# Two-way instead of four-way interleaving of a chunk's columns, and layer 1 in batches of eight blocks

## The chip, the cores and the metric

The kernel runs on one core of one Trainium2 chip. Its time is device microseconds (us) of that core. TensorE (PE) multiplies, VectorE (DVE) and ScalarE (ACT) do the elementwise work, GpSimd (POOL) does a few powers and adds, and SyncE (SP) issues the transfers. "PEld" in the profile is TensorE's loading of weights, the stationary operand of a matmul.

## What is computed

There are 4096 nodes with 64 features, and a dense adjacency matrix of 4096 x 4096 float32 (64 MB) of which somewhat under one entry in a hundred is not zero. Cut to what matters:

```python
# layer 0, two hops
h = relu(layernorm(x)); g = h
for k in range(2):
    g = tanh(concat([adj @ g, g], axis=1) @ W[k])
x = x + g
# layer 1
h = relu(layernorm(x))
mask = adj != 0
rank = cumsum(mask, axis=1); deg = rank[:, -1:]; k = minimum(deg, 100)
w = mask * where(rank - (deg - k) > 0, 0.5 ** (deg - rank), 0)
x = x + w @ (h @ weight) + bias
```

So layer 0 needs the matrix twice (once for each hop), and layer 1 needs, for each entry that is not zero, how many such entries stand to its right in its row.

## The kernel before, in words

**Chunks, blocks and the order of columns.** The rows of the matrix are cut into four *row chunks* of 1024 (I, or g, or J where it is the source of layer 1), and its columns into 32 *blocks* of 128 source nodes. The host lays the matrix out so that `adjA[I, b]` is one transfer of 128 source nodes by 1024 target nodes of chunk I, 512 KB. On the chip the 1024 target nodes of a chunk are two halves of 512 columns (c). A half holds four *tiles* t of 128 nodes, and its column number is 4 p + t for node p of tile t: the four tiles are interleaved. A chunk's features stand in two forms: transposed, 128 partitions (half, feature) by 512 columns in that order, and by nodes. Going from the first to the second is a transpose on TensorE: `nodes` (L198) takes each tile's 128 columns out of the transposed form as the weights of a matmul against the identity (L202). In memory the columns of a tile are thus four float32 elements apart. The way back is `features_T` (L249), whose copy `hT` (L258) writes with the same step. `nodes` is called eight times: for x1 of each chunk in the first sweep, in `finish_row` (L297), and for x2 of each chunk in the second, in `finish_x2` (L409).

**Sweep 1** (L325) reads the whole matrix for the first hop. DVE also makes of every block a byte code per entry (`count_pair`, L211), which stays on the chip, and the aggregation runs as `agg_pair` (L232) or, for blocks whose second hop can be done from the same read, as full-width matmuls (L362).

**Sweep 2** (L611) reads the rest of the matrix again for the second hop (L658 to L660). In the stretch that matters here it reads into four slots of `ring`, so a block's transfer can start only when the block four places before it has been multiplied. A block costs two matmuls of `agg_pair`, side by side in the two halves of the array's columns.

**Layer 1** runs in between and after. Its work is 64 *units* (J, g, n), in the order of `units` (L463): source chunk J = 3, 2, 1, 0, target chunk g = 0 to 3, and n = 0 to 3 for pairs of source blocks. Each unit is first decoded to bf16 powers of two: `convert` (L468) widens its bytes, on ACT (two of L488) or on DVE (L479 and L482), and `add_base` adds a row of counts on DVE (L501). Then `layer1(n)` (L532) takes n units: for all of them the matmuls with the high parts of the features (L549, weights 128 wide, four for each unit), and then for all of them those with the low part (L560, weights 64 wide in the two column halves, four for each unit). It is called with 2. The sums of four units (one J and g) gather in one accumulator of PSUM, and after the fourth `layer1` reads it out: for J = 3 with copies (L572), for J = 2 and 1 with three adds on DVE (L578), for J = 0 with three adds into temporaries (L586), which `finish_out` (L592) multiplies with the weights (L193, "pf"), copies (L596), transposes by nodes (L602, "pto"), adds to the residual (L607) and stores. In layer 1 the two halves of a unit's columns are the even and the odd ones, so L602 picks columns two elements apart. The temporaries come from a pool of five buffers.

**What sets the order.** All engines work in program order, and the program is written out by a planner: `clock` (L388) holds an estimated time of each engine, `decode` (L513) issues conversions and adds as long as their engine's clock is at most `lead` ahead of TensorE's, and `due` (L635) says how many units are to be done after so many blocks of sweep 2, so that 36 of the 64 are due by its end. `while state["done"] + 2 <= due(n + 2)` (L674) issues batches between the blocks; L696 to L698 does so after the last block. The lead is 5.0 in the sweep, 2.5 after it and 8.0 once chunk 0 of x2 is ready (L683 to L686). `finish_x2` (L394) makes a chunk's features for layer 1 in steps: matmul (L193), add and tanh, transpose (L202), residual (L410), layer norm (L152 to L163, with a power on POOL, L158), split into bf16 parts (L425 to L429). Units of source chunk J wait for that of chunk J.

Of the kernel before, what the change touches and what calls it, by code (L numbers as in the profile page):

```python
# [16 lines left out]
P = 128  # L17
# [14 lines left out]
def gnn_kernel(  # L32
# [21 lines left out]
    nc = tc.nc  # L54
# [4 lines left out]
    CB = 8  # L59
    NCH = NB // CB  # L60
# [3 lines left out]
    TC = C // P  # L64
# [31 lines left out]
    def tmp(shape=None, dtype=F32, name="tmp"):  # L96
        return tpool.tile(shape or [P, C], dtype, tag="tmp", name=name)

    def one(name="one"):
        return pone.tile([P, C], F32, tag="one", name=name)  # L100

    def two(name="two"):
        return pone.tile([P, C], F32, tag="two", name=name)
# [26 lines left out]
    ident = cpool.tile([P, P], F32, name="ident")  # L130
# [53 lines left out]
            nc.scalar.activation(hx[:, b0 + i, :D], xc[:, i, :], AF.Relu, scale=s[:, i : i + 1])  # L184


    by_t = lambda ap: ap.rearrange("q (p t) -> q t p", t=TC)

    def paired(po, terms):

        for n, (w, v) in enumerate(terms):
            for c in range(NC):
                nc.tensor.matmul(  # L193
                    po[c * D : (c + 1) * D, :], w(c), v(c),
                    start=n == 0, stop=n == len(terms) - 1,
                )

    def nodes(src):  # L198

        pt = one(name="pt")  # L200
        for t in range(TC):
            nc.tensor.matmul(  # L202
                pt[:, t * P : (t + 1) * P], by_t(src)[:, t, :], ident,
                start=True, stop=True, skip_group_check=True,
            )
        return pt.rearrange("p (t c e) -> p t c e", t=TC, c=NC)
# [33 lines left out]
    def step():  # L240
        while steps:
            try:
                next(steps[0])
                return
            except StopIteration:
                steps.pop(0)


    def features_T(I):  # L249
        pt = one(name="ph")  # L250
        for t in range(TC):
            for c in range(NC):
                nc.tensor.matmul(
                    pt[c * D : (c + 1) * D, t * P : (t + 1) * P],
                    hx[:, CB * I + c * TC + t, :D], ident, start=True, stop=True, skip_group_check=True,
                )
        hT = tmp(name="hT")
        nc.scalar.copy(by_t(hT), pt.rearrange("q (t p) -> q t p", t=TC))  # L258
        return hT

    def own_share(I):
# [7 lines left out]
    def finish_row(I, acc, held):  # L269
# [25 lines left out]
        nc.scalar.activation(x1T, x1T, AF.Tanh)  # L295
        yield
        pt = nodes(x1T)  # L297
        for c in range(NC):
            nc.tensor.matmul(
# [77 lines left out]
    def late_weights():  # L377
        for h in range(2):
            nc.sync.dma_start(wz[h * D : (h + 1) * D, h, 0, 0], weight)
        nc.sync.dma_start(  # L380
            wz[:, 0, 0, 1],
            bass.AP(tensor=bias.tensor, offset=bias.offset, ap=[[0, P], [1, D]]),
        )
# [6 lines left out]
    def use(engine, us, after=0.0):  # L390
        clock[engine] = max(clock[engine], after) + us
        return clock[engine]
# [49 lines left out]
    def space(ap, t=0.0):  # L442
        if not any(ap is g for g in gone):
            spaces.append((ap, t))
# [15 lines left out]
    def ring_space(s):  # L460
        return quad(ring[:, s, :].bitcast(I16))

    units = [(J, g, n) for J in range(NCH - 1, -1, -1) for g in range(NCH) for n in range(CB // 2)]  # L463
    ready = {}
    made = []
    state = {"added": 0, "done": 0, "acc": None, "lead": 5.0}
# [125 lines left out]
    def finish_out(g, ys):  # L592
        po = one(name="pf")
        paired(po, [(lambda c: wa, lambda c: ys[c]), (lambda c: wz[:, c, 0, 0], lambda c: ys[2])])
        oT = tmp(name="oT")
        nc.scalar.copy(oT, po)  # L596
        yield use("ACT", 0.6, use("PE", 1.9) + 0.1)
        pt = two(name="pto")
        v = oT.rearrange("q (c p j) -> q c j p", c=2, j=2)
        for c in range(2):  # L600
            for j in range(2):
                nc.tensor.matmul(  # L602
                    pt[:, (c * 2 + j) * P : (c * 2 + j + 1) * P], v[:, c, j, :], ident,
                    start=True, stop=True, skip_group_check=True,
                )
        o = tmp(name="o")
        nc.vector.tensor_add(o, pt, flat(pre1[:, chunk(g), :]))  # L607
        nc.sync.dma_start(ov[:, chunk(g), :], o.rearrange("p (t e) -> p t e", e=D))
        use("DVE", 0.7, use("PE", 1.3) + 0.2)

    def sweep2():  # L611
        ring_all = list(range(RING))
        early = pacc.tile([P, 3, C], F32, tag="acc", name="acc1")
        accs = {2: early[:, 0, :], 3: early[:, 1, :]}
        plan = [(2, 16, 24), (3, 24, 32), (2, 24, 32), (1, 8, 32), (0, 8, 32)]
        blocks = [(I, b) for I, b0, b1 in plan for b in range(b0, b1)]
        space(quad(mbuf.rearrange("p a r i -> p (a r i)").bitcast(I16)))

        h0_space = hm[:, : 2 * CB, : 2 * D].bitcast(I16).rearrange("p (r k b) d -> p r k b d", r=2, k=2)
        free = {s: 0.0 for s in ring_all}  # L620
        slots = ring_all
        chain = []
        total = len(blocks)
        n_late = 7 * CB // 2

        def run_chain(now):
            if chain and chain[0][0] <= now:
                t, gen = chain.pop(0)
                t = next(gen, None)
                if t is not None:  # L630
                    chain.insert(0, (t, gen))
                return True
            return False

        def due(done_blocks):  # L635

            if done_blocks <= 24:
                return 0
            return (len(units) - n_late) * (done_blocks - 24) / (total - 24)

        seq = 0
        for n in range(0, total, 2):
            I, b = blocks[n]
            if n == 8:
                while steps:
                    step()
                late_weights()
            if n == 24:
                slots = ring_all[:4]
                for s in ring_all[4:]:  # L650
                    space(ring_space(s), free[s])
            if I not in accs:
                accs[I] = two(name="acc1")
            for r in range(2):
                s = slots[seq % len(slots)]
                seq += 1
                a = ring[:, s, :]
                nc.sync.dma_start(a, adjA[I, b + r])  # L658
                landed = use("DMA", 1.33, free[s]) + 2.2
                agg_pair(accs[I], hx[:, b + r, D:], a, b + r == max(CB * I, CB), b + r == NB - 1)  # L660
                free[s] = use("PE", 0.9, landed)
            if steps:
                step()
            if n == 8:
                space(h0_space, clock["PE"])
            if b + 2 == NB and I == 1:
                gone.append(h0_space)
                spaces[:] = [v for v in spaces if v[0] is not h0_space]
            if b + 2 == NB:
                gen = finish_x2(I, accs[I])  # L670
                chain.append((next(gen), gen))
            run_chain(clock["PE"])
            decode()
            while state["done"] + 2 <= due(n + 2):  # L674
                J = units[state["done"]][0]
                if J not in ready or ready[J] > clock["PE"] + 1.0:
                    break
                layer1(2)
                run_chain(clock["PE"])
                decode()  # L680
        for s in slots:
            space(ring_space(s), free[s])
        state["lead"] = 2.5  # L683
        while state["done"] < len(units) or chain or outs:
            if 0 in ready:
                state["lead"] = 8.0  # L686
            if run_chain(clock["PE"]):
                decode()
                continue
            if outs and outs[0][0] <= clock["PE"]:  # L690
                t, gen = outs.pop(0)
                t = next(gen, None)
                if t is not None:
                    outs.insert(0, (t, gen))
                continue
            i = state["done"]  # L696
            if i < len(units) and units[i][0] in ready and ready[units[i][0]] <= clock["PE"] + 1.0:
                layer1(2)  # L698
                decode()
                continue  # L700
            decode()
            later = [x[0] for x in chain[:1] + outs[:1]] + [t for t in ready.values()]
            clock["PE"] = min(t for t in later if t > clock["PE"])

    sweep1()
    sweep2()


# [24 lines left out]
```

## Time and profile before

| | us |
|---|---|
| three runs | 442.91, 443.53, 444.13 |
| median | 443.53 |
| the profiled execution, its own time | 443.52 |
| its span, first to last instruction | 441.7 |
| TensorE busy | 389.2 |
| VectorE busy | 321.9 |
| ScalarE busy | 144.2 |
| granted TensorE clock, mean | 0.954 of full speed |

The span is what the profile's pieces add up to; some 1.8 us of the execution's time lie outside it. Durations below are of this one execution. The "chain of work" is followed back from the last instruction, at each step to what released it, so that its pieces have no gaps between them. In the stage list the columns are the busy time of each engine in a stretch, with the number of instructions in brackets, then the granted clock of TensorE, the share of the transfer engines, and GB/s.

### The profile page before, as it was taken

Reading aid. Unit: us, or ns where it says so; the run is one execution under the profiler, and the core shown is the slowest. Engines: PE = TensorE matmul, PEld = TensorE weight load, DVE = VectorE, ACT = ScalarE, POOL = GpSimd, SP = SyncE. Lnnn points to the kernel's source line nnn. Section 1 sums busy time; section 2 is a strip of 40 time slices with the busy share of each in tenths; the row PEclk is TensorE's granted clock in tenths of the full one; section 3 lists DMA queues with packets and bytes.
Section 4 is the critical chain, followed back from the end, with each engine's and each line's share of the span. In section 5 each row is a group of like instructions: output and inputs, shape, how many; then the busy total and the mean of one; then the engine's idle time right before and its main releaser. Section 6 shows DMA issues by size and latency. Waiting matters only on the chain.

```text
span 441.7 us, 4685 instructions
## 1 busy us (share of the span) xinstructions
PE 389.2 (88%) x1636; PEld 148.4 (34%) x1636; DVE 321.9 (73%) x547; ACT 144.2 (33%) x231; POOL 26.2 (6%) x21
## 2 busy tenths in 40 slices
PE   3748699988999999999979778599999999968995
PEld 0213234312443444444423132333343333422342
DVE  3899965499989997997703045657779999799932
ACT  2134532100120003000043031416457698549810
POOL 1133200000000000000000020030002100020000
PEclk9669989999999999999999898979999999996998
DMA  7999920999999964888499979048866872000011
GB/s 264 409 329 415 406 96 0 347 411 408 410 410 408 407 243 157 302 317 301 160 347 312 391 272 334 16 155 304 299 223 247 281 244 104 2 0 1 0 47 49
DMA packets 31736, 108.54 MB, mean 246 GB/s; under 512 B 4449, under 2 KB 4705, under 8 KB 31713
## 3 DMA queue, kind: packets, MB, share of 16 engines
q1 hardware_dynamic: 31712, 108.25, 65.8%
q8 instruction: 13, 0.21, 0.2%
q14 instruction: 11, 0.08, 0.1%
HBM read 107.18 MB, written 1.05 MB: 245 GB/s over the span
## 4 chain that ended last, share of the span: by engine, by line
PE 70%; DMA 15%; DVE 8%; ACT 3%; POOL 2%; issue 1%; SPq 0%; DVEq 0%; ACTq 0%
PE acc L232 20%; PE acc L362 19%; PE accl L549 12%; DMA ring<-in_adjA_dram 10%; PE accl L560 6%; PE pt L202 4%; PE po L193 3%; DMA codes<-in_adjA_dram 3%; DVE mbuf L215 2%; PE pf L193 2%; DMA pre<-in_x_dram 1%; ACT junk L179 1%; POOL s L181 1%; DVE codes L225 1%; PE pto L602 1%
## 5 line engine op out<-in xcount | busy, mean ns | idle before, releaser
L232 PE MATMUL acc<-ring,hx 128*64 128x512 f32 x456 | 116.5, 639 | 27.2 <-DMA ring<-in_adjA_dram 10.0
L232 PEld LDWEIGHTS acc<-ring,hx 128*64 128x64 f32 x456 | 31.7, 144 | 95.5 <-issue 42.4
L362 PE MATMUL acc<-ring,hx 128*128 128x512 f32 x144 | 62.4, 593 | 0.2 <-DMA ring<-in_adjA_dram 0.2
L232 PE MATMUL acc<-codes,hx 128*64 128x512 f32 x184 | 46.5, 632 | 14.3 <-ACT hx L184 11.4
L225 DVE TENSOR_TENSOR codes<-mbuf,lo 128x512 uint16<-128x512 uint16 x124 | 52.7, 425 | 4.2
L215 DVE TENSOR_SCALAR mbuf<-ring 128x2048 uint8<-128x2048 f32 x37 | 45.2, 1221 | 4.2 <-DMA ring<-in_adjA_dram 4.2
L488 ACT ACTIVATE codes<-codes 128x1024 int16<-128x1024 uint8 x48 | 46.8, 1042 | 1.0 <-PE accl L560 1.0
L226 DVE TENSOR_SCALAR lo<-codes 128x512 uint16<-128x512 uint16 x128 | 37.6, 294 | 4.5
L549 PEld LDWEIGHTS <-hx 128*128 128x128 bf16 x256 | 23.6, 101 | 51.3 <-issue 25.8
L271 ACT COPY S<-acc 128x512 f32<-128x512 f32 x4 | 2.3, 586 | 117.6 <-PE acc L362 116.5
L362 PEld LDWEIGHTS acc<-ring,hx 128*128 128x128 f32 x144 | 27.3, 190 | 34.7 <-issue 33.2
L215 DVE TENSOR_SCALAR mbuf<-codes 128x2048 uint8<-128x2048 f32 x27 | 33.0, 1220 | 7.0 <-DMA codes<-in_adjA_dram 6.9
L501 DVE TENSOR_TENSOR codes<-codes,base 128x2048 uint16<-128x2048 int16 x31 | 36.9, 1220 | 0.1
L158 POOL TENSOR_TENSOR s<-s,half 128x8 f32<-128x8 f32 (+2 forms) x6 | 10.5, 1758 | 338.5 <-DVE s L157 338.5
L549 PE MATMUL accl<-codes,hx 128*128 128x512 bf16 x124 | 30.5, 380 | 0.0
L488 ACT ACTIVATE ring<-codes 128x1024 int16<-128x1024 uint8 x30 | 29.7, 1046 | 0.1
L501 DVE TENSOR_TENSOR ring<-ring,base 128x2048 uint16<-128x2048 int16 x20 | 24.5, 1247 | 5.5 <-ACT ring L488 5.5
L232 PEld LDWEIGHTS acc<-codes,hx 128*64 128x64 f32 x184 | 12.9, 144 | 45.7 <-issue 23.2
L549 PE MATMUL accl<-ring,hx 128*128 128x512 bf16 x80 | 21.6, 405 | 5.7 <-DVE hx L428 5.7
L362 PE MATMUL acc<-codes,hx 128*128 128x512 f32 x48 | 21.2, 594 | 0.0
L560 PEld LDWEIGHTS <-lo 128*64 128x64 bf16 x256 | 11.9, 110 | 20.8 <-issue 13.6
L560 PE MATMUL accl<-codes,lo 128*64 128x512 bf16 x124 | 17.4, 385 | 0.0
(98 smaller groups left out, 331.7 us busy)
## 6 DMA issues: line engine op xcount, KB each, us to landing
ring<-in_adjA_dram SPq DMA_DIRECT2D x146, 512.0 KB, 5.6
codes<-in_adjA_dram SPq DMA_DIRECT2D x54, 512.0 KB, 9.7
xres<-in_x_dram SPq DMA_DIRECT2D x4, 256.0 KB, 6.4
out_dram<-o SPq DMA_DIRECT2D x4, 256.0 KB, 2.5
pre<-in_x_dram SPq DMA_DIRECT2D x3, 256.0 KB, 8.4
pre<-in_x_dram SPq DMA_DIRECT2D x1, 192.0 KB, 6.5
wz<-in_W_dram SPq DMA_DIRECT2D x4, 32.0 KB, 7.3
pre<-in_x_dram SPq DMA_DIRECT2D x1, 64.0 KB, 2.1
```

The lines of the kernel that those rows point to most:

```text
L158: nc.gpsimd.tensor_tensor(s2, s2, half[:, :nb], op=ALU.pow)
L193: nc.tensor.matmul(po[c * D : (c + 1) * D, :], w(c), v(c), start=n == 0, stop=n == len(terms) - 1,)
L202: nc.tensor.matmul(pt[:, t * P : (t + 1) * P], by_t(src)[:, t, :], ident, start=True, stop=True, skip_group_check=True,)
L215: nc.vector.tensor_scalar(m, a, 0.0, float(FLAG - 1), op0=ALU.not_equal, op1=ALU.mult)
L225: nc.vector.tensor_tensor(q, m[:, r].bitcast(U16), cnt, op=ALU.add)
L226: nc.vector.tensor_scalar(cnt, q, 0x7F7F, None, op0=ALU.bitwise_and)
L232: nc.tensor.matmul(acc[c * D : (c + 1) * D, :], src, a[:, c * C : (c + 1) * C], start=first, stop=last,)
L362: nc.tensor.matmul(acc[:, c, :], hx[:, g, :], a[:, r, c * C : (c + 1) * C], start=g == CB * I - 1, stop=g == 0,)
L488: nc.scalar.activation(w[:, r], src[:, r].rearrange("p (x y k) -> p k x y", k=2, x=X), AF.Copy, scale=float(FLAG))
L501: nc.vector.tensor_tensor(w.bitcast(U16), w, bg[:, None, :].to_broadcast([P, 2, CW]), op=ALU.add)
L549: nc.tensor.matmul(like(accs[-1][:, c, :], w), hm[:, CB * J + 2 * k + r, : 2 * D], w[:, r, c], start=k == 0 and r == 0, stop=k == CB // 2 ...
L560: nc.tensor.matmul(like(acc[c * D : (c + 1) * D, 2, :], w), lo[:, CB * J + 2 * k + r, :], w[:, r, c], start=k == 0 and r == 0, stop=k == C ...
```

## The change

The order of columns in a half becomes 256 u + 2 p + v, with tile t = 2 u + v: two tiles are interleaved instead of four. The host's layout of the matrix, `nodes` and `features_T` follow. In layer 1 the even and odd columns then hold, for each, two whole tiles one after the other, so L602 picks columns that stand side by side. For J = 2, 1 and 0 `layer1` is called with four units (eight blocks, all of one J and g) instead of two; for J = 3 still with two. The planner's estimates are unchanged, but it now issues a batch only when four units are due.

```diff
-    by_t = lambda ap: ap.rearrange("q (p t) -> q t p", t=TC)
+    by_t = lambda ap: ap.rearrange("q (u p v) -> q u v p", u=2, v=2)
...
-                pt[:, t * P : (t + 1) * P], by_t(src)[:, t, :], ident,
+                pt[:, t * P : (t + 1) * P], by_t(src)[:, t // 2, t % 2, :], ident,
...
-        nc.scalar.copy(by_t(hT), pt.rearrange("q (t p) -> q t p", t=TC))
+        nc.scalar.copy(by_t(hT), pt.rearrange("q (u v p) -> q u v p", u=2, v=2))
...
-        v = oT.rearrange("q (c p j) -> q c j p", c=2, j=2)
+        v = oT.rearrange("q (c j p) -> q c j p", c=2, j=2)
...
+        def batch():
+            return 2 if units[state["done"]][0] == NCH - 1 else CB // 2
...
-            while state["done"] + 2 <= due(n + 2):
+            while state["done"] < len(units) and state["done"] + batch() <= due(n + 2):
                 J = units[state["done"]][0]
                 if J not in ready or ready[J] > clock["PE"] + 1.0:
                     break
-                layer1(2)
+                layer1(batch())
...
-                layer1(2)
+                layer1(batch())
...
-    adjA = np.asarray(adj).reshape(128, 4, 2, 4, 128, 32).transpose(1, 5, 4, 2, 0, 3)
+    adjA = np.asarray(adj).reshape(128, 4, 2, 2, 2, 128, 32).transpose(1, 6, 5, 2, 3, 0, 4)
```

Built, the changed kernel has as many matmuls, transfers and POOL instructions as before; some conversions move from DVE to ACT. The order on TensorE is the same up to the end of the last batch of J = 3.

## The prediction, made before the changed kernel had run

> **What bounds the kernel now.** I read the page's busy shares and chain first, then the busy times by stage, then the chain piece by piece, then the timelines of VectorE and of the transfers.
>
> ```profile
> PE 389.2 (88%) x1636; PEld 148.4 (34%) x1636; DVE 321.9 (73%) x547; ACT 144.2 (33%) x231; POOL 26.2 (6%) x21
> ...
> PE 70%; DMA 15%; DVE 8%; ACT 3%; POOL 2%; issue 1%; SPq 0%; DVEq 0%; ACTq 0%
> ```
>
> TensorE makes 70% of the chain. The stages from the last quarter of the span on:
>
> ```profile
> core 0: us, PE busy (x) PEld busy (x) DVE busy (x) ACT busy (x) POOL busy (x), PEclk, DMA share, GB/s
> 286.00:320.00 34.00, 33.61 (x162) 11.61 (x164) 23.57 (x35) 15.54 (x19) 3.79 (x2) 0.91 0.71 244
> 320.00:371.00 51.00, 50.94 (x261) 18.68 (x258) 46.71 (x64) 39.57 (x44) 4.46 (x2) 1.00 0.69 240
> 371.00:399.30 28.30, 22.57 (x127) 9.70 (x126) 24.26 (x35) 15.25 (x19) 2.88 (x2) 0.97 0.00 1
> 399.30:437.40 38.10, 37.36 (x192) 15.30 (x192) 25.77 (x31) 19.93 (x23) 0.00 (x0) 0.93 0.06 22
> ```
>
> TensorE is full in all but the third, where it waits some 5.7 us for chunk 0 of x2. But DVE is 46.7 of 51 us busy in the second: it has little room for waits of its own. In the chain, a transpose, the two phases of a batch, blocks, and the next batch:
>
> ```profile
> 328.88 2.06 PE pt L202 x8
> 330.94 1.73 PE accl L549 x8
> 332.66 0.98 PE accl L560 x8
> 333.65 1.72 PE acc L232 x8
> 335.36 1.83 PE accl L549 x8
> ```
>
> (Start, us, what; x8 at L202 is four float32 matmuls of two passes each, at L232 two blocks of 0.86.) The same transpose from weights two elements apart:
>
> ```profile
> 420.49 1.14 PE pto L602 x8
> ```
>
> How DVE waits, and how long two block transfers take that are issued together:
>
> ```profile
> 380.36 1.89 DVE L578 TENSOR_TENSOR codes<-accl,codes 128x512 f32<-128x512 f32 x3 [2.12 <-PE accl L560]
> ```
> ```profile
> ring<-in_adjA_dram SPq DMA_DIRECT2D x1, 512.0 KB, 3.2
> ```
> ```profile
> ring<-in_adjA_dram SPq DMA_DIRECT2D x1, 512.0 KB, 5.4
> ```
>
> L578 stood 2.12 us at the head of DVE's queue until the batch's last L560 was done. The transfers are those issued near 359.1 and 359.9: 3.2 us to landing for the first, 5.4 for the second (4.5 in other pairs).
>
> [...] L202's weight loads take 327 ns, L602's 196, and L362's, contiguous, 190. [...] L549 takes 1.83 after 64-wide work and 1.73 after the 128-wide transpose, so 0.10; L560 takes 0.98 against half of 1.73, so 0.115. [...] after 5.73 idle the batch at 399.27 ran its first eight matmuls in 3.57 instead of 1.83. [...]
>
> **The change part by part.**
>
> *1. Transposes by nodes.* Eight calls, 2.06 to 1.14 each (L602's row, the same shape): -0.92 x 8 = -7.4. All eight lie in the chain. Bounds: 0 if the step isn't what slows them, -7.4.
>
> *2. L602 and hT.* L602's loads go from two elements apart to contiguous: 32 x (196-190) ns = -0.2 at most; taken as 0. hT (1.10 us, 0.59 if contiguous) is waited for by 0.8 us in all; ACT is on the chain there only behind other work. 0, between 0 and -0.8. The host's layout moves the same 512 KB a block: 0. SP and POOL keep their order.
>
> *3. Fewer mode switches.* 48 units in 12 batches instead of 24: 12 x (0.10+0.115) = -2.6. A batch of four costs 5.4 instead of 5.62.
>
> *4. Runs of six blocks on four slots.* The changed order has three runs of six blocks between batches (12 matmuls of L232 in a row), where before no run had more than four. In a run the fifth block's slot is free 0.86 after the start; issue 0.1, 3.2 to landing: there at 4.2, wanted at 3.44. The sixth: free at 1.72, landing 4.5 to 5.4 after issue: 6.3 to 7.2, wanted at 5.0. The run ends at 7.2 to 8.0 instead of 5.16: +2.4 each, +7.3. Before had one such wait, 0.45 at 365. Net +6.9. Were both landings at 3.2, it would be +2.4 in all; at the queue's worst (6.0) +10.
>
> *5. DVE's queue up to chunk 0.* The read-out (L578) of a batch stands in DVE's order ahead of adds (L501, 1.17 each) for the next batch, or the one after. I laid the changed order out by hand, with 5.4 a batch, 0.86 a block, 1.15 a transpose, 1.9 a read-out, 1.17 an add, 0.85 a conversion on DVE, 2.0 on ACT. Zero is the end of the last J = 3 batch (319.96 before). The second J = 2 batch waits for its third and fourth unit (residual and layer norm of x2 stand ahead): +0.95. The next two are supplied. After the sweep three J = 1 batches run on; the third ends at 72.35. Only then can its read-out go (to 74.3), then an add (75.5), L156 and L157 (76.4), two adds (77.6, 78.8): these three adds are the units two to four of the last J = 1 batch, which TensorE had begun at 72.35. It ends at 81.6 instead of 77.75: +3.85. Then its read-out (83.6), one add (84.8), L161, L163, L425, L427, L428: chunk 0 ready at 87.9, 6.3 after the batch against 5.73 before: +0.6. Together +5.4. Nothing covers this: TensorE has no other work then. If DVE's pieces overlap by a fifth it is +4; POOL and DVE together (L161 took 1.1 there) can add 1.
>
> *6. Chunk 0's units.* Before, eight units beyond its own four were added ahead of the first L586, and TensorE ran through: 38.2 us from 399.27 to the last L607. Changed, that L586 stands in DVE's order after the first four units only, and five adds follow it. From chunk 0's readiness: first batch to 7.75 (cold, as before). L586 waits for it, three of 0.63 to 9.75, first add 10.95: TensorE idle 3.2; the second batch takes its units at 1.17 instead of 0.87 each and ends at 17.25. pf to 19.1; the third of the next L586 needs a temporary that pf frees, so the adds come at 20.45, 21.6, 22.8: the third batch ends at 25.5. pto, pf, fourth batch: 34.0. Then pto, pf, oT, pto, pf, oT, pto in a row, two copies of 0.7 exposed: last L607 at 42.6. Net +4.4; this holds 0.9 of the gain of part 3, so +5.3 beside it. Bounds +2 (L586 of the first two columns at the end of the L549 phase; at 380.36 it wasn't so) and +10 (clock, below).
>
> Sum: -7.4 - 2.6 + 6.9 + 5.4 + 5.3 = +7.6. Against the profiled execution, 443.52 (span 441.7 and 1.82 around it; the median of the runs is 443.53): **451.1**, I say 451.
>
> **Rivals.** *A, faster: DVE's queue does not hold TensorE.* Place: read-outs ahead of the next batch's adds, parts 5 and 6. Price without them: -10.0 + 6.9 = 440.4. It decides from parts 5 and 6 together under 3.1 us. For it: before, the same queue kept eight units ahead in the last stage, and the longer waits for blocks give DVE time. Against: strict order, and L578 at 380.36. 0.14.
>
> *B, slower still: the clock.* With 3.2 idle in part 6 and then short bursts, TensorE may fall to half speed for the second and third batches: a unit's four matmuls take 1.72 (0.43 each, as after 399.27) against adds at 1.17, +2.4 each: 456. [...] 0.12.
>
> *C, the change doesn't do what it says:* two elements apart is fast at L602 for another reason and L202 stays at 2.06: +7.4, 458.5. Same engine, operands and shape speak against it. 0.04.
>
> *D, between:* waits of parts 4 to 6 half covered, 443 to 445. 0.04.
>
> **How the numbers follow.** The forecast, parts 1 to 6 as summed, 0.66, with its own range 446.5 to 455: part 4 at +2.4 for the low end, upper bounds of 5 and some of 6 for the high. Leaving out A and C (0.18), the range is 443.5 to 457. Within 0.3% (442.2 to 444.9, about what a measurement of this kernel can tell from no change) is D and a little of the forecast's edge: 0.05. Faster 0.14, slower 0.81.
>
> **What would show it.** L202's weight loads near 196 ns and x8 at 1.14 (part 1, C); L549 and L560 in runs of 16 at about 3.55 and 1.85 (part 3); in three runs of L232 x24 waits on ring loads of 2 to 3 us (part 4); L549 waiting on L501, not on the batch before, before 399 by 4 us, and by 3 us at the second J = 0 batch with DVE idle ahead of L586 (5, 6); the granted clock after it (B). Wrong it would be if waits of L549 on L501 sum to under 3 us, or if DVE is found adding units ahead of the read-outs.

## The result, and the profile after

| | median, us | runs, us | ratio to before, 95% interval |
|---|---|---|---|
| before | 443.65 | 442.91 to 444.13 | |
| changed, first time | 458.3 | 452.63, 458.01, 458.6, 459.25 | 1.0305 [1.022, 1.039] |
| changed, once more | 456.35 | 453.39 to 457.54 | 1.0279 [1.0206, 1.0351] |

The changed kernel is slower by 12 to 15 us, where +7.6 was forecast; 451 was too low and the median lies above the top of the range, 457 (the second median just below it). Some executions are disturbed and come out longer; the medians here and below leave them out, and since the profiled execution of the first time was one of them (461.92; another took 991.84), the profile read here is that of the second: own time 457.53, span 455.0, against 443.52 and 441.7.

The page's busy shares and the chain by engine:

```profile
PE 387.9 (85%) x1636; PEld 143.2 (31%) x1636; DVE 318.3 (70%) x541; ACT 147.8 (32%) x237; POOL 25.4 (6%) x21
...
PE 63%; DMA 19%; DVE 10%; ACT 3%; issue 2%; POOL 1%; SPq 1%; ACTq 0%; DVEq 0%
```

TensorE has hardly less to do (387.9 for 389.2), but it makes 63% of the chain and not 70%; transfers went from 15 to 19% of it, DVE from 8 to 10%, ACT stayed at 3%. Most of the transfers' rise lies ahead of the late stages, in the part of the chain up to 314 us (19% there before, 25% now), so these shares don't say what the change did. The stages do, cut at the same events as before: the end of the last J = 3 batch, the end of the sweep's last block, the first batch of J = 0:

```profile
core 0: us, PE busy (x) PEld busy (x) DVE busy (x) ACT busy (x) POOL busy (x), PEclk, DMA share, GB/s
281.00:315.00 34.00, 32.62 (x162) 11.26 (x164) 24.55 (x37) 16.53 (x20) 3.79 (x2) 0.92 0.69 240
314.90:372.50 57.60, 50.77 (x246) 17.82 (x242) 39.77 (x55) 36.70 (x42) 2.90 (x2) 0.94 0.61 215
372.50:406.80 34.30, 25.41 (x142) 10.82 (x141) 26.48 (x38) 16.06 (x20) 3.79 (x2) 0.93 0.00 1
406.80:450.70 43.90, 38.60 (x192) 16.09 (x192) 27.43 (x31) 27.44 (x31) 0.00 (x0) 0.90 0.05 18
```

In the first column that counts, the length: 51.0 became 57.6, 28.3 became 34.3, 38.1 became 43.9. The last part of the sweep was full (50.94 of 51.00) and now has 6.8 us of gaps, at a clock of 0.94 and not 1.00. The two stages after it have more gaps too. Only the beginning is shorter: the last J = 3 batch ends at 315.1, before at 320.0. One pair of units, 2.8 us of work, also went from the second stage to the third: the second holds 16 units where it held 18.

The chain after the last J = 3 batch, before, and ACT's copy of chunk 1's sums (S, L398) in the same profile:

```profile
319.96 1.72 PE acc L232 x8
321.68 1.83 PE accl L549 x8
323.51 0.98 PE accl L560 x8
324.49 0.95 PE po L193 x4
325.44 3.43 PE acc L232 x16
```
```profile
323.73 0.58 ACT L398 COPY S<-acc 128x512 f32<-128x512 f32 x1
```

The same piece after:

```profile
315.12 0.59 ACT codes L572
...
316.95 2.00 ACT ring L488 x2
318.95 0.48 ACT S L398
319.44 0.04 issue
319.48 5.35 PE acc L232 x16
324.83 0.86 PE po L193 x4
325.69 3.56 PE accl L549 x16
329.25 1.87 PE accl L560 x16
```

Before, this stretch was TensorE without a break. Now the chain leaves it for ACT: read-outs of J = 3, two conversions (L488), and the copy S, which four blocks wait for. These then take 5.35 us; 16 matmuls of L232 took 3.43 before. Below that, a batch of four in 3.56 + 1.87.

The weight loads of four of the transposes by nodes, as a group that keeps shapes apart (operation, count, busy, mean ns of one):

```profile
L202 PEld LDWEIGHTS pt<-ident,y 128*128 128x128 f32 x32 | 4.1, 196 | 2.0 <-issue 1.2 <-ACT y L406 0.8
```

196 ns for a weight load, where L202 had 327. And the DVE queue at the last J = 1 batches and at chunk 0's first read-out (start, us, instruction, in brackets the idle time before and its releaser):

```profile
390.75 1.89 DVE L578 TENSOR_TENSOR codes<-accl,codes 128x512 f32<-128x512 f32 x3 [1.38 <-PE accl L560]
392.56 1.22 DVE L501 TENSOR_TENSOR ring<-ring,base 128x2048 uint16<-128x2048 int16 x1
...
394.48 2.37 DVE L501 TENSOR_TENSOR ring<-ring,base 128x2048 uint16<-128x2048 int16 x2
...
415.10 1.89 DVE L586 TENSOR_TENSOR yo<-accl,codes 128x512 f32<-128x512 f32 x3 [4.30 <-PE accl L560]
416.90 3.49 DVE L501 TENSOR_TENSOR codes<-codes,base 128x2048 uint16<-128x2048 int16 x3
```

DVE stands idle at the head of its queue (1.38, 4.30) while the adds behind it are what TensorE wants next. TensorE's side of these waits, and of the blocks before them:

```profile
346.11 1.08 PE L232 MATMUL acc<-ring,hx 128*64 128x512 f32 x4 [0.87 <-DMA ring<-in_adjA_dram]
347.52 1.08 PE L232 MATMUL acc<-ring,hx 128*64 128x512 f32 x4 [0.34 <-DMA ring<-in_adjA_dram]
...
358.28 1.08 PE L232 MATMUL acc<-ring,hx 128*64 128x512 f32 x4 [0.84 <-DMA ring<-in_adjA_dram]
361.04 1.85 PE L232 MATMUL acc<-ring,hx 128*64 128x512 f32 x4 [1.68 <-DMA ring<-in_adjA_dram]
...
393.82 1.02 PE L549 MATMUL accl<-ring,hx 128*128 128x512 bf16 x4 [2.14 <-DVE ring L501]
395.76 3.35 PE L549 MATMUL accl<-ring,hx 128*128 128x512 bf16 x8 [0.91 <-DVE ring L501]
...
406.81 1.87 PE L549 MATMUL accl<-ring,hx 128*128 128x512 bf16 x4 [5.86 <-DVE hx L428]
...
418.18 4.66 PE L549 MATMUL accl<-codes,hx 128*128 128x512 bf16 x12 [3.12 <-DVE codes L501]
```

These are the waits of the second and third run of six blocks (part 4) and of parts 5 and 6, each where it was expected. (Ends of matmuls in such lists are modelled and reach some 0.17 past the next start.)

Put beside the forecast, by stage. Each number is a difference of lengths between the two profiles:

| stage | forecast | measured | missed |
|---|---|---|---|
| up to the last J = 3 batch (six of the transposes) | -5.5 | -4.9 | 0.6 |
| from there to the last block | +3.2 | +6.5 | 3.3 |
| to chunk 0's first batch | +5.5 | +5.9 | 0.4 |
| to the last L602 | +4.4 | +5.8 | 1.4 |
| together | +7.6 | +13.3 | 5.7 |

The forecast of the second row is made of part 4 (+6.9), the wait of 0.95 from part 5, one transpose (-0.9), and four batches of four units where nine pairs stood (-3.7). The third row takes up the pair that moved (+2.0 with the cheaper batches), has a transpose (-0.9) and the rest of part 5 (+4.4).

### The profile page after: what moved, and what is told of

Read it like the earlier page. It is cut to its first block, busy times and chain, and to the rows that moved or that the text cites. A ratio compares the mean times of both kernels' runs of the same rounds, so it can differ in the third digit from the quotient of the medians.

```text
span 459.8 us, 4671 instructions
## 1 busy us (share of the span) xinstructions
PE 386.9 (84%) x1619; PEld 144.1 (31%) x1636; DVE 318.6 (69%) x541; ACT 147.7 (32%) x237; POOL 26.5 (6%) x21
## 4 chain that ended last, share of the span: by engine, by line
PE 62%; DMA 17%; DVE 11%; ACT 4%; issue 3%; POOL 2%; SPq 0%; ACTq 0%; DVEq 0%
PE acc L362 18%; PE acc L232 17%; DMA ring<-in_adjA_dram 12%; PE accl L549 11%; PE accl L560 6%; PE po L193 3%; DMA codes<-in_adjA_dram 3%; DVE mbuf L215 2%; PE pt L202 2%; DVE codes L501 1%; DMA pre<-in_x_dram 1%; DVE codes L578 1%; PE pf L193 1%; ACT junk L179 1%; POOL s L181 1%
## 5 line engine op out<-in xcount | busy, mean ns | idle before, releaser
L232 PE MATMUL acc<-ring,hx 128*64 128x512 f32 x456 | 120.0, 656 | 36.8 <-DMA ring<-in_adjA_dram 16.7
L232 PEld LDWEIGHTS acc<-ring,hx 128*64 128x64 f32 x456 | 31.6, 147 | 109.2 <-issue 42.6
L362 PE MATMUL acc<-ring,hx 128*128 128x512 f32 x144 | 62.4, 593 | 0.2 <-DMA ring<-in_adjA_dram 0.2
L232 PE MATMUL acc<-codes,hx 128*64 128x512 f32 x184 | 46.9, 637 | 15.7 <-ACT hx L184 12.9
L488 ACT ACTIVATE codes<-codes 128x1024 int16<-128x1024 uint8 x54 | 52.6, 1042 | 4.4 <-issue 3.4
L549 PEld LDWEIGHTS <-hx 128*128 128x128 bf16 x256 | 24.8, 103 | 58.3 <-issue 24.5
L362 PEld LDWEIGHTS acc<-ring,hx 128*128 128x128 f32 x144 | 27.3, 190 | 34.7 <-issue 33.2
L501 DVE TENSOR_TENSOR codes<-codes,base 128x2048 uint16<-128x2048 int16 x31 | 36.8, 1220 | 0.8 <-ACT codes L488 0.8
L549 PE MATMUL accl<-codes,hx 128*128 128x512 bf16 x119 | 33.1, 413 | 4.3 <-DVE codes L501 4.0
L488 ACT ACTIVATE ring<-codes 128x1024 int16<-128x1024 uint8 x30 | 29.7, 1045 | 0.0
L549 PE MATMUL accl<-ring,hx 128*128 128x512 bf16 x76 | 20.9, 402 | 9.7 <-DVE hx L428 5.9
L501 DVE TENSOR_TENSOR ring<-ring,base 128x2048 uint16<-128x2048 int16 x20 | 24.6, 1248 | 5.5 <-ACT ring L488 5.5
L578 DVE TENSOR_TENSOR codes<-accl,codes 128x512 f32<-128x512 f32 x24 | 15.1, 684 | 17.9 <-PE accl L560 17.9
L232 PEld LDWEIGHTS acc<-codes,hx 128*64 128x64 f32 x184 | 12.8, 144 | 46.8 <-issue 20.8
L362 PE MATMUL acc<-codes,hx 128*128 128x512 f32 x48 | 21.2, 594 | 0.0
L294 DVE TENSOR_TENSOR x1T<-po,pre 128x512 f32<-128x512 f32 x4 | 2.8, 692 | 25.2 <-PE po L193 25.2
```

The costliest lines, as they stand in the source:

```text
L232: nc.tensor.matmul(acc[c * D : (c + 1) * D, :], src, a[:, c * C : (c + 1) * C], start=first, stop=last,)
L362: nc.tensor.matmul(acc[:, c, :], hx[:, g, :], a[:, r, c * C : (c + 1) * C], start=g == CB * I - 1, stop=g == 0,)
L488: nc.scalar.activation(w[:, r], src[:, r].rearrange("p (x y k) -> p k x y", k=2, x=X), AF.Copy, scale=float(FLAG))
L501: nc.vector.tensor_tensor(w.bitcast(U16), w, bg[:, None, :].to_broadcast([P, 2, CW]), op=ALU.add)
L549: nc.tensor.matmul(like(accs[-1][:, c, :], w), hm[:, CB * J + 2 * k + r, : 2 * D], w[:, r, c], start=k == 0 and r == 0, stop=k == CB // 2 ...
L578: nc.vector.tensor_tensor(p, acc[:, q, :], p, op=ALU.add)
```

## The experiments

Times of whole runs of these kernels spread by about 1% around their medians, and the early part of the program, the same in all that share a layout, ended up to 6.8 us apart in their profiles (at 313.0 in one, at 319.8 in that of the layout alone, whose profiled execution is the longest of its four). Where a verdict needs less than that it rests on stage lengths from the traces. These repeat better: the stretch to the last block, the same program in three of the kernels, took 57.1, 57.5 and 58.0 us, so a difference of under one microsecond between stages of single profiles proves little. The three late stages of the table, from the block behind the last J = 3 batch to the last L602, are together 117.6 us before and 135.8 in the changed kernel; these lengths are called "the late part" below. The main theory: each part costs or gives on its own, and the time that the forecast lacked lies in waits of TensorE that were priced too low. The rivals: the new layout also slows something (the parts are not additive), or one shortage (DVE, or transfers) has merely moved from place to place, so that mending one wait brings another.

### Each half of the change alone

`layout_only`: the new order of columns, all batches of two.

```diff
-            return 2 if units[state["done"]][0] == NCH - 1 else CB // 2
+            return 2
```

> The new order of columns, with layer 1 in batches of two units everywhere, as before. If the layout does only what part 1 says (eight transposes, 0.92 us each): 443.6 - 7.4 = 436.2 us, with the transposes at 1.14. Rival: the layout costs in the first sweep what it saves, since in the changed kernel's trace the work common to both ends 0.66 us later in spite of six cheaper transposes: then 443 to 447, with the first transpose of x1 2 to 3 us later than the kernel before has it.

`batches_only`: the new batches, the old order of columns (the five lines of the layout put back).

> The old order of columns, with batches of four units for J = 2, 1 and 0. If the gains and losses of the two parts add up: about 458.3 (the changed kernel) + 7.4 = 466. If the layout is what costs: 458 or less.

`after_again` is the changed kernel once more, beside them.

> The changed kernel once more, for its spread (452.6 to 461.9 in the runs so far) and a second trace. If the delay before the last J = 3 batch (6 us against the sum) is chance, of when the clock is granted, it differs in this trace; if it belongs to the layout, it is there again. About 457.

Measured: layout alone 436.54 (ratio 0.9849 [0.9787, 0.991]); batches alone 465.18 (1.0482 [1.0416, 1.0548]); both 456.35; before, beside them, 443.76. The layout gives 7.2 us and the batches take some 21; 436.54 + 465.18 - 443.76 = 457.96 is what two independent halves would make together, and 456.35 to 458.3 was measured. Part 1 stands; the error lies with the batches, in parts 4 to 6. The delay ahead of the last J = 3 batch that `after_again` asks about was chance: that batch ends at 320.5 in the first profile of the changed kernel and at 314.9 in the second. No kernel below is faster than the layout alone. In the batches alone, with the old columns, the new wait is there as well:

```profile
326.37 5.35 PE L232 MATMUL acc<-ring,hx 128*64 128x512 f32 x16 [2.69 <-ACT S L398]
```

### Batches of four for one source chunk only

`four_at_J2`, and later `four_at_J1`:

```diff
-            return 2 if units[state["done"]][0] == NCH - 1 else CB // 2
+            return CB // 2 if units[state["done"]][0] == 2 else 2
```

> The new order of columns; batches of four for J = 2 only, of two for J = 1 and 0. It has the three runs of six blocks (part 4) and the wait of the second J = 2 batch, not parts 5 and 6 proper. By the recorded sum: 436.2 + 6.9 + 0.95 - 0.9 = 443.1. By the changed kernel's trace, where this stretch holds 12.7 us of waits and slow clock against 0.45 before: 436.2 + 11.3 = 447.5. If the read-outs in VectorE's queue were the whole loss: 437.

> The new layout with batches of four for J = 1 only. If part 5 is right and separate, the waits of the last J = 1 batch (3.3 us in sum in the changed kernel's traces) are there again, and those of J = 2 and 0 are not: 436.5 + 3.4 - 0.9 = 439. If they come from the batches of J = 2 before: 436.

Measured: J = 2 alone 448.65 (1.0108 [1.0031, 1.0185]), 12.1 over the layout alone. From the end of the last J = 3 batch to chunk 0's first batch the trace has 87.2 us; with the layout alone it has 78.0 (77.9 in the profile of `layout_filled` below, the same program up to there), with the whole change 91.9. So J = 2 is 9.3 of the 13.9 us that this stretch grew by, and that is where the forecast was 3.3 short. J = 1 alone: the trace has 81.8, +3.9, with waits on L501 of 1.28 and 0.91. That it costs so much as a rule is not shown: the profiled execution is the longest of its four (443.73), the four matmuls behind these waits took 1.87 us in it and 1.02 in `two_then_four` behind the same waits, and the whole time, 437.2 (0.9841 [0.9781, 0.99]), can't be told from that of the layout alone. J = 0 alone wasn't tried; what is left of the whole for it is the last stage, 43.9 against 37.9, +6.0.

### A batch left in the place where the wait arose

`two_then_four`: twos until the first twenty units are done, then fours.

```diff
-            return 2 if units[state["done"]][0] == NCH - 1 else CB // 2
+            return 2 if state["done"] < 5 * CB // 2 else CB // 2
```

> The changed kernel with batches of two also for the first four units of J = 2: a batch then stands again between the last block of chunk 1 and the first of chunk 0, and the first run of six blocks is gone. If the wait there is for the bank of PSUM that chunk 1's sums hand over to chunk 0's (2.7 us for its copy on ScalarE, and a slow clock after it, 1.8 us), with the transfers of the run's end: 457.5 - 5 = 452.5. If only the transfers of that run cost, as the recorded sum has it (2.4): 455. If VectorE's queue is the whole loss: 457.

This puts two short batches where the changed kernel has one of four, so that one of them stands again between chunk 1's last block and chunk 0's first. TensorE then:

```profile
315.50 1.88 PE L232 MATMUL acc<-ring,hx 128*64 128x512 f32 x8
317.32 0.82 PE L549 MATMUL accl<-ring,hx 128*128 128x512 bf16 x3
...
320.07 1.08 PE L193 MATMUL po<-S,wz 128*64 128x512 f32 x4
320.98 3.60 PE L232 MATMUL acc<-ring,hx 128*64 128x512 f32 x16
```

No wait on S, and the four blocks at full speed. The stretch to the last block is 51.5 us and not 57.5. The later waits became shorter as well, for the edit also moves the batches behind it to other places among the blocks (on L501 in the last J = 1 batch 1.28 instead of 2.14): the late part is 126.1, 9.7 less. The whole time, 451.43 (1.0222 [1.0141, 1.0302]), is 9.5 over the runs of before beside it (441.91), where the changed kernel had 12.6 over its own; its runs reach from 447.66, the profiled one, to 454.25. The sign agrees, the whole amount is seen in the trace only.

### ACT's queue ahead of the copy

`copy_free`: units 20 and 21, whose conversions stood ahead of S on ACT, are converted on DVE.

```diff
-        if max(clock["ACT"], t) + 2.0 > max(clock["DVE"], t) + 2.2:
+        if i in (20, 21) or max(clock["ACT"], t) + 2.0 > max(clock["DVE"], t) + 2.2:
```

> The changed kernel, with units 20 and 21 converted on VectorE instead of ScalarE, so that no conversion stands in ScalarE's queue ahead of the copy of chunk 1's sums; the run of blocks stays. If the handed-over bank is what TensorE waits for, and ScalarE's order is why so long: the wait of 2.69 falls to about 1 and the four blocks after it may run at full clock: 1.7 to 3.5 us less, 454 to 456. If those blocks wait for transfers underneath: the same time, with the wait moved to ring loads.

```profile
320.00 1.94 PE L232 MATMUL acc<-ring,hx 128*64 128x512 f32 x8 [1.73 <-ACT S L398]
```

The wait shrinks from 2.69 to 1.73, and two blocks after it take 1.94 as listed (1.88 without a wait): no slow clock. The edit moved one thing more on TensorE: chunk 1's L193 now stands between these two blocks and the next two. The stretch to the last block is 52.6, 4.9 less. So the copy behind ACT's queue is what TensorE waits for, and the wait is dear because of what follows it. The whole time doesn't settle it: 453.99 (1.0291 [1.023, 1.0353]) is 2.4 below the changed kernel in us and level with it as a ratio. The profiled run's early part ended 1.5 later, which hides some of the gain.

### Adds ahead of read-outs

`adds_ahead_last` issues the adds for the next four units before the first L586; `adds_ahead_J1` does it before L578 of J = 1, g = 2 (the tuple is then `(1, 2)`).

```diff
+        while units[todo[0]][:2] == (0, 0) and state["added"] < min(todo[-1] + 5, len(units)):
+            if len(made) <= state["added"]:
+                convert()
+            add_base()
         for i, acc in zip(todo, accs):
```

> The changed kernel, with the adds of the next four units put ahead of the first read-out of J = 0 in VectorE's order, and nothing moved on TensorE. If the order on VectorE is what holds TensorE there (part 6): the idle of 3.1 us ahead of the second J = 0 batch is gone and that batch is not paced by adds: 3 to 5 us less, 453.5. If TensorE waits there for something else (ScalarE's conversions, temporaries, the read-out itself): the same time.

> The changed kernel, with the adds of the last four units of J = 1 put ahead of the read-out before them (part 5), nothing moved on TensorE. If that order is the cause of the waits of 2.15, 0.91 and less in the last J = 1 batch: 3 to 3.9 us less, 454, and chunk 0 ready 5.8 us after that batch as before. If the layer norm of chunk 0 sets the end of that stage anyway: the waits turn up ahead of the first J = 0 batch instead, and the time stays.

At the second J = 0 batch, and at the last J = 1 batch (a fence for each kernel):

```profile
412.89 2.76 PE L549 MATMUL accl<-codes,hx 128*128 128x512 bf16 x12
415.98 1.02 PE L549 MATMUL accl<-ring,hx 128*128 128x512 bf16 x4 [0.32 <-DVE ring L501]
```

```profile
392.76 1.02 PE L549 MATMUL accl<-ring,hx 128*128 128x512 bf16 x4 [0.70 <-DVE ring L501]
394.66 1.02 PE L549 MATMUL accl<-ring,hx 128*128 128x512 bf16 x4 [0.87 <-DVE ring L501]
...
404.02 0.58 PE L549 MATMUL accl<-ring,hx 128*128 128x512 bf16 x1 [6.50 <-DVE hx L428]
```

In the first, the 3.12 is gone, twelve matmuls take 2.76 instead of 4.66 as listed, and the last stage is 40.2 and not 43.9. The late part is 131.8, 4.0 less. Whole time 453.21 (1.0287 [1.0214, 1.0361]). In the second, 2.14 and 0.91 became 0.70 and 0.87, and the stretch to chunk 0's first batch is 32.1 and not 34.4; 0.64 of the gain is given back in front of chunk 0 (6.50 for 5.86). The late part is 133.1, 2.7 less. Whole time 452.96 (1.0238 [1.0165, 1.0312]). Both times are 3 us below the changed kernel's 456.35 and only 1 to 2 nearer to their own runs of before, 441.91. Parts 5 and 6 thus had the right cause: not that DVE has too much to do, but that a read-out stands ahead of adds. In part 5 this is about half of the wait; the 1.57 us that stay come from elsewhere, most likely from waits of the adds themselves for ACT's conversions, as the first kernel has them (DVE idle 0.67 ahead of each of three).

### All three mended

`mended` has the batches of `two_then_four` and the adds ahead at `(0, 0)` and `(1, 2)`.

> The changed kernel with three of its waits taken away together: batches of two for the first four units of J = 2, and the adds of the next four units ahead of the read-out both at the end of J = 1 and at the first batch of J = 0. The traces of the single edits have the stretch up to the last block 6.0 us shorter, the one up to chunk 0's readiness 2.3, the last 3.4 (3.0 to 3.7 by which trace it is set beside). If these are separate: 457.5 - 11.7 = 446, with the two later runs of six blocks and the rest of the waits as what is left over the layout alone (436.5). If one wait takes another's place: over 449.

Measured: 444.77 against 443.67 (1.002 [0.9993, 1.0046]), so the three mends bring some 11.5 us, level with before. In the traces the late part is 121.2, 14.6 less than in the changed kernel; the single mends made it shorter by 9.7, 4.0 and 2.7, together 16.4. The waits are mostly separate, and the rival of one shortage that moves on falls. An overlap of some 2 us is left to it, all of it in the last stage, which the single mends shorten by 1.4, 3.7 and 0.9 and the three together by 3.7. Against the layout alone (115.9) the late part is still 5.3 longer: 1.0 up to the last block, where the last run of six still waits 0.64 and 1.59 for transfers, 2.1 up to chunk 0, and 2.3 after it.

### The clock after a wait

`after_filled` is the changed kernel with matmuls on constants in the three places where TensorE waits: 22 ahead of chunk 0's block 8, 40 ahead of its first batch in layer 1, 26 ahead of the second. Their result is not used.

```diff
+    def fill(n):
+        junk = one(name="junk")
+        for _ in range(n):
+            nc.tensor.matmul(junk[:, : 2 * P], tri, ident.bitcast(BF16), start=True, stop=True)
```

`layout_filled` is the layout alone with the 40 ahead of chunk 0.

> The changed kernel with matmuls of constants into an unused bank put where TensorE waits: 22 of them (2.4 us at full clock) ahead of the first block of chunk 0, 40 ahead of the first J = 0 batch, 26 ahead of the second. They add work and nothing to the result. If a wait of 2.7 us costs the clock for some 3.5 us after it: the four blocks there take 3.5 instead of 5.35, the first J = 0 batch about 5.5 instead of 7.5, the matmuls of the second 3.6 instead of 4.45: 4 to 5 us less, 453. If the slow blocks wait for something else: the same or slower.

> The new layout with batches of two, and 40 matmuls of constants where TensorE waits for chunk 0 of x2 (6.3 us in that trace). If the half clock after that wait is what makes the first batch take 3.57 and part of the next: 436.5 - 1.8 to 2.6 = 434. If the fill delays the batch: 437 or more.

The hand-over to chunk 0 in the first of them:

```profile
318.22 2.58 PE L390 MATMUL junk<-ident,tri 128*128 128x256 bf16 x22
320.97 3.65 PE L232 MATMUL acc<-ring,hx 128*64 128x512 f32 x16 [0.18 <-ACT S L403]
```

The wait for S is as long as before, now with work in it, and the four blocks run in 3.65 as listed and not 5.35; the stretch to the last block is 2.4 shorter and the last stage 2.4. The late part is 131.0, 4.8 less; whole time 453.52 (1.0222 [1.0156, 1.0288]). So the slow blocks come from the idleness, not from the blocks or their data. In the layout alone the same means gains nothing, 437.66 (0.986 [0.9813, 0.9908]), although its first J = 0 batch now runs at full speed; some batches later TensorE meets a wait for DVE:

```profile
406.44 1.89 PE L556 MATMUL accl<-codes,hx 128*128 128x512 bf16 x8 [2.30 <-DVE yo L593]
```

(L593 is that kernel's read-out.) What the batch saves, the wait for DVE takes: 37.9 us for the stage with and without.

## Why the prediction was wrong

The direction and five of six mechanisms were right, and the size was not: 451 forecast, 456.35 and 458.3 measured.

**Part 1** was right: 196 ns a weight load, 1.14 a call, and 7.2 us in the layout alone where 7.4 was forecast. Of the three steps that the traces hold, a load took 327 ns at four elements, 196 at two, and contiguous 190 (L362) or 191 (L602 in the changed kernel). **Part 2**: hT fell from 1.10 to 0.62, still two elements apart, and nothing else moved. **Part 3**: 3.56 and 1.87 for a batch of four, as forecast. A mode switch, from 128-wide to 64-wide weights or back, stands in that trace as about 0.10 us: a unit's L549 take 0.86 from start to start, the last ahead of L560 0.96; a unit's L560 take 0.43 to 0.45, the last ahead of L202 0.53.

**Part 4 failed**, and in it the first of the three runs. It priced all three by transfers alone, +2.4 each. The first run is not six blocks of one chunk: after two blocks chunk 1 ends and chunk 0 begins. Their sums use the same buffer (`two`, L653), so chunk 0's first matmul must wait until ACT has copied chunk 1's out (L398). That dependence was in the kernel before, where ACT's copy ended at about 324.3 and TensorE was busy with a batch until 324.5 (L193, which needs S too, didn't wait): covered by the very batch that the change moves behind the blocks. I counted what a run of six does to the transfers, and didn't ask what the batch inside it had been hiding. The price is a wait of 2.69 and then 1.92 (5.35 - 3.43), nearly all slow clock, 4.6 for the 2.4; the transfers, waited for meanwhile, cost nothing there. Two short batches in that place removed it, less work ahead of the copy shortened it, and constant matmuls in it took away the slow clock alone.

The other two runs: from the first block to the end of the sixth 6.9 and 9.0 us against 5.16, so +1.7 and +3.8 where +2.4 each was forecast, together 0.7 more. The longer one had waits of 0.84 and 1.68, after which its last matmuls took 1.85 for four and the next batch's first unit 1.68: the clock again, some 1.7 us, of which half lies in the next batch. So the stretch's miss of 3.3 is, but for rounding, 2.2 in the first run, 0.7 in the other two, and 0.8 in the batch behind, less 0.5 because the wait forecast at 0.95 in part 5 was 0.42.

**Part 5** was right in the main: 2.14 and 0.91 before the second and third unit of the last J = 1 batch, 3.05 in all, +5.9 for +5.5. That batch took 10.3 us and not 9.25, since its last eight matmuls of L549 ran in 3.3 us (1.73 in an undelayed batch). Chunk 0 was then ready after 5.86 (5.73 before) and not 6.3, which gave part of that back. **Part 6** was right in its cause (3.12 idle for the 3.2 forecast, DVE idle ahead of L586) and short by 1.4: the second batch ended 18.6 after its stage began and not 17.25, because three of its units ran at a slow clock, 4.49 us with 0.62 granted, rather than at the pace of the adds. That is rival B's mechanism, over sooner than B had it: only one batch was hit, so it cost 1.3 and not 5. The forecast had given B only 0.12, taking 3.2 us of idle time as still too short, which no trace had shown: in that of before, 20 matmuls of L232 behind a wait of 2.25 (at 264.16) took 6.22 us with 0.72 granted, and here 2.69 was enough. Rivals A and C are excluded by the waits and by L202. That the measured times stand nearest to the figures of B (456) and C (458.5) is chance: C's mechanism was absent, and most of what was missing lay in neither's place.

The range failed with part 4: its upper bound, +10, covered transfers only, and no case for a wait other than theirs was worked out. The remaining 0.6 up to the last J = 3 batch lies within what that part of the program varies by between profiles.

## What to carry to other kernels

When a change moves a piece of work out from between two others, first list every dependence between those two (a buffer that is handed over, a copy queued on another engine), because the piece may have been hiding it. Batches that are larger save little here (0.2 us each) and ask for more adds between one read-out and the next, so ahead of such a change look at what stands in the same queue behind the step that waits for the batch. And price a long TensorE wait as more than its length: here single waits of 1.73 and 2.30 us in the late part cost only themselves, those of 2.69 us 1.4 to 1.8 us of slow matmuls on top, and one of 2.25 us earlier in the sweep (before, at 264.16) about as much.

## What the runs showed of the hardware

After a single wait of 2.69 us, the next four blocks took 5.0 to 5.35 us as listed, for 3.60 without a wait, in each of the kernels that had it (granted clock 0.68 over them in the changed one); with the idle time filled they took 3.65, at 1.00. After 3.12 us, twelve matmuls of L549 took 4.40 to 4.66 for 2.76. After single waits of 1.73 (`copy_free`, clock 1.00) and 2.30 (`layout_filled`) nothing was lost. But earlier in the sweep, in the trace of before, a wait of 2.25 was enough:

```profile
264.16 6.22 PE L232 MATMUL acc<-ring,hx 128*64 128x512 f32 x20 [2.25 <-DMA ring<-in_adjA_dram]
```

The clock over these matmuls was 0.72; at the pace above (3.60 for four blocks, 0.86 for one more) they would have taken some 4.46.

Shorter waits in a row went either way. After 2.14 and 0.91, eight matmuls took 3.35 (changed kernel) and 3.57 (`batches_only`) for 1.90; after 1.28 and 0.91, four took 1.02 in one kernel and 1.87 in another; after 0.84 and 1.68, 1.85 for 1.08 (0.79 over the next batch's matmuls), after 0.98 and 1.27, or 0.64 and 1.59, still 1.08. What decides, there and between the single waits, was not tested.

The copy that writes with a step shows a price that rises with the step: 1.10 us at four elements (hT before), 0.62 at two, and 0.59 for a copy of the same shape without one (L302).
